# Layer 1 of a two-layer graph and mixture-of-experts kernel: rows kept in token order, pages found by an inverted permutation, and more rules in the event model that orders the instructions

## The chip, the cores and the metric

The program runs on one core of one Trainium2 chip. Its time is the device time of one execution in microseconds (us). The core has TensorE (PE in the profile; PEld is its weight load), VectorE (DVE), ScalarE (ACT), GpSimd (POOL) and SyncE (SP), each with a queue of instructions that it takes in order, and 16 DMA engines that serve SP's queue and POOL's.

## The reference, cut to what matters

Two layers, each a graph attention over 2708 nodes of 256 features and then a mixture of experts in which each node (token) goes to two experts. The change touches the second mixture (16 experts, hidden width 512):

```
x = x + L1_gnn(layernorm(x), adj)
xn = layernorm(x)
logits = xn @ gate_w + gate_b                  # [2708, 16]
topk_vals, topk_idx = top_k(logits, 2)
topk_w = softmax(topk_vals)
h = relu(xn @ w1[e] + b1[e])                   # for the two chosen experts e
moe = sum over the two of topk_w * (h @ w2[e] + b2[e])
x = x + layernorm(xn + moe) * gamma + beta
```

## The kernel before, in words

**Tokens, groups, pages.** The 2708 tokens lie in 22 tiles of 128 rows (the last two hold 74 rows each). In layer 1 they pass the router in four groups, tiles 0 to 5, 6 to 11, 12 to 17 and 18 to 21 (`groups1`). An expert's tokens are gathered in *pages* of 128 rows, each page belonging to one expert; there are at most 58 pages, and the first 45 (`SURE1`) are computed without a test, the others only if they are used. A page is called a block when it is computed, and `where[0]` and `where[1]` say for each block which expert and which page it is.

**Layer 1's attention.** After the projections, for each token tile `i` TensorE sums 22 x 2 matmuls (`sum_up`, L1773) over masks that are stored in fp8 and widened to fp32r by GpSimd or ScalarE, one half of a tile at a time (`widen`, a cast of 128 x 1408 elements, L1621 and L1623). `finish1` and `points1` then make the tile's output `x1`, its layernorm and the normalized row `router1.rows[t]`, a buffer of 259 numbers (256 features, the token's number, a mark of its first expert, and the difference of its two top logits). `logits1` turns two tiles and multiplies them with the gate.

**Routing a group** (`route1`, L2114 on). `pick` finds each token's two experts on VectorE, and GpSimd copies the three trailing numbers into the rows (L671). `rank` counts, by matmuls with triangular and all-one matrices, how many tokens of the same expert come earlier; `number` (VectorE, L710 to L746) turns this into `place`, each token's page and slot as one number. Then `scatter1` (L753) has GpSimd write every tile's rows to their places in DRAM (`rows_d`, 58 x 128 rows), by two indirect DMAs a tile, one for each expert of the token; `plan` (L881 to L948) works out, on VectorE, TensorE and ScalarE, the owners and numbers of the pages that have become full, and the biases.

**The experts** (`Experts.stream`). For each block SP loads the page's 128 rows with one direct DMA at a register's address (`fetch`, L848 to L850) and the expert's weights (L834, L838), unless the block four before had the same expert. TensorE turns the rows (L515), does 16 matmuls for the hidden layer (L972) and nine for the output (L987, L990), ScalarE the relu (L976), VectorE the weight of the token (L964, L994) and the scaled output (L996). GpSimd adds the output's rows to DRAM by an indirect DMA that accumulates (L1001). Blocks of the first group of pages (8 pages, known when tiles 0 to 11 are routed) come first, then 12 pages of tiles 0 to 17, then the rest. The last three blocks are not added in DRAM but joined by matmuls.

**What sets the order.** The instructions of layer 1 from the attention on are emitted in an order that a small event model makes when the program is built (`Clock`): each strand of work is a generator that yields an engine and a duration, or a mark to wait for, and the model always goes on with the strand that can start first, the smaller `urgency` first when two can start together. The order is then fixed; an engine waits in its queue for whatever instruction is at the head. The model knows how long an instruction takes, 0.25 us for a handover between engines, a queue of DMAs, and slots for buffers (13 row buffers `xrs`, five PSUM banks `bank`, three more `acc`, four widened masks). It does not know that SP takes its instructions in order.

Of the kernel before, what the change touches and what calls it, by code (L numbers as in the profile page):

```python
# [64 lines left out]
class Clock:  # L65
# [3 lines left out]
    HANDOVER = 0.25  # L69

    def __init__(self):
        self.now, self.free, self.pieces = 0.0, {}, []

# [21 lines left out]

    def run(self):
        while self.pieces:
            best = None
            for entry in self.pieces:
                ready, urgency, _, want, had = entry  # L100
                if isinstance(want, Mark):
                    if want.at is None:
                        continue
                    key = (max(ready, want.at), -1)
                else:
                    if had not in (None, want[0]):
                        ready += self.HANDOVER
                    key = (max(ready, self.free.get(want[0], 0.0)), urgency)
# [7 lines left out]
            else:  # L116
                entry[4], us, *latency = entry[3]
                entry[0] += us
                self.free[entry[4]] = entry[0]
# [28 lines left out]
def kernel(  # L148
# [381 lines left out]
    for t in (TF, LAST):  # L530
# [12 lines left out]
    tri = filled("tri", 1.0, P, BF16)  # L543
    nc.gpsimd.affine_select(out=tri, in_=tri, pattern=[[1, P]], compare_op=OP.is_gt,
                            fill=0.0, base=0, channel_multiplier=-1)
    ones_bf = filled("ones_bf", 1.0, P, BF16)
# [3 lines left out]
    page_start = counted("page_start", [[0, 1]], 0, P, 1)  # L550
    page_end = counted("page_end", [[0, 1]], P, P, 1)
    of_32 = const.tile([P, 1], F32, name="of_32")
    for k in range(0, P, 32):
        nc.gpsimd.iota(of_32[k:k + 32], pattern=[[0, 1]], base=0, channel_multiplier=1,
                       allow_small_or_imprecise_dtypes=True)
# [13 lines left out]
    class Router:  # L569
# [4 lines left out]
        def __init__(self, layer, E, groups, w_gate, b_gate, pool):  # L574
            self.w_gate, self.b_gate, self.E, self.layer = w_gate, b_gate, E, layer
            self.blocks = NB = blocks_of(E)
            self.rows_d = dram.tile([NB * P, RW], F32, name=f"rows_d{layer}")
# [170 lines left out]

        def scatter(self, t, r):
# [46 lines left out]
    class Experts:  # L796
# [49 lines left out]
        def fetch(self, b):  # L846
            xg = self.xg_tile(b)
            start = nc.values_load(where[1][0:1, b:b + 1], engines=[ET.SP], min_val=0,  # L848
# [13 lines left out]
        def plan(self, upto, bank=None):  # L862

            R, NB, lo, v = self.router, self.NB, self.planned, nc.vector
            E, G, n = R.E, len(R.groups), upto - self.planned

            def small(name, dtype=F32, cols=1):
                return row.tile([P, cols], dtype, name=name, tag=name, bufs=1)[:NB]
# [5 lines left out]
            def give_back(slot):  # L874
                if slot:
# [3 lines left out]
            junk, ones = small("ended", cols=max(len(pairs) * E0, len(groups1) * E1)), ones_bf[:NB]  # L879
            yield SMALL  # L880
            v.scalar_tensor_tensor(junk[:, :G], R.ends[:NB, :, E - 1], page_start[:NB],  # L881
                                   ones[:, :G], op0=OP.is_le, op1=OP.mult, accum_out=whole)
            yield "DVE", 0.2, 0.09
            v.scalar_tensor_tensor(junk[:, :G * E], R.ends[:NB].rearrange("p g e -> p (g e)"),
                                   page_start[:NB], ones[:, :G * E], op0=OP.is_le, op1=OP.mult,
# [5 lines left out]
            if upto == NB:  # L891
                v.tensor_scalar(fresh, self.taken[:NB], -1.0, 1.0, op0=OP.mult, op1=OP.add)
            else:

                open_ = small("open")
                v.scalar_tensor_tensor(junk[:, :E], R.page[:NB], page_end[:NB], ones[:, :E],
                                       op0=OP.is_equal, op1=OP.mult, accum_out=open_)
                yield SMALL
                v.scalar_tensor_tensor(fresh, page_start[:NB], R.ends[:NB, R.done - 1, E - 1:], open_,
                                       op0=OP.is_lt, op1=OP.subtract)  # L900
                yield SMALL
                v.tensor_tensor(fresh, fresh, self.taken[:NB], OP.subtract)
# [5 lines left out]
            nc.tensor.matmul(ps[:NB, :32], tri[:NB, :NB], fresh_bf.to_broadcast([NB, 32]),  # L908
# [3 lines left out]
            v.tensor_scalar(at, ps[:NB, :1], float(lo), None, op0=OP.add)  # L912
            yield "DVE", 0.23, 0.09
            v.scalar_tensor_tensor(sel, self.order[:NB, lo:upto], at, fresh.to_broadcast([NB, n]),
                                   op0=OP.is_equal, op1=OP.mult, accum_out=used)
            v.tensor_tensor(self.taken[:NB], self.taken[:NB], used, OP.add)
            give_back(slot)
            ps, slot = yield from bank_of("where_ps")
            yield "PE", 0.7
            for k, what in enumerate((owner, page_start[:NB])):  # L920
# [1581 lines left out]
```

## Time and profile before

| | us |
|---|---|
| median of 3 runs (lowest, highest) | 1133.14 (1131.94, 1135.37) |
| the profiled execution | 1137.78 |
| its span, first to last instruction | 1136.1 |
| PE busy in the span | 1039.2 (91%) |
| DVE, ACT, POOL busy | 545.7, 577.9, 368.7 |
| DMA moved | 234.38 MB, mean 206 GB/s |

The profile is of one execution. Its second part divides the span into 40 slices of 28.4 us; a digit is the busy share of a slice in tenths, and PEclk is the clock that TensorE was granted, in tenths of full speed. Layer 0's attention fills slices 3 to 11, its experts slices 12 to 23, layer 1's projections slices 24 and 25, its attention slices 26 to 31, the first blocks, beside the routing of the last groups, slices 32 to 34, the other blocks slices 35 to 39, and the last slice is the output. A table by stretches gives for each engine the busy time and, behind an x, the number of instructions. A timeline lists instructions in order of time, like ones merged, with the idle time of the engine before the first of them in brackets, and what ended it: "issue" where the profile shows nothing that it waited for, "remote" where a semaphore ended the wait and no instruction is seen that set it then.

### The profile page before, as it was taken

What the parts mean: (1) busy time and instruction counts of PE and PEld (TensorE: products, weight loads), DVE (VectorE), ACT (ScalarE), POOL (GpSimd) and SP (SyncE); (2) the same over time, 40 slices, a digit from 0 to 9 for tenths busy, and PEclk for the clock granted to TensorE, in tenths of its full rate; (3) what the DMA queues carried; (4) which work ended last, traced back from release to release, by engine and by line L of the source; (5) the groups of instructions that cost most, each with busy time, mean ns of one, the idle gap of its engine ahead of it and who ended that gap; (6) DMA issues with size and microseconds to landing.
All of it is one profiled execution on the core that took longest, in us unless ns stands there. A gap on an engine that the chain in (4) does not pass through costs nothing. (4 is left out here: it accounts for less than half of the span.)

```text
span 1136.1 us, 21474 instructions
## 1 busy us (share of the span) xinstructions
PE 1039.2 (91%) x6707; PEld 922.6 (81%) x6707; DVE 545.7 (48%) x2210; ACT 577.9 (51%) x1602; POOL 368.7 (32%) x425
## 2 busy tenths in 40 slices
PE   5999999998989999999999999898994957999984
PEld 3888888887879999999999954898983846999873
DVE  7788888886431110011001347578775643122257
ACT  4876767665434444444444446445653522444454
POOL 7531113111242211222123271352623155443350
PEclk9999999999989999999999999999997878999998
DMA  9955444431888999999899959301215645685893
GB/s 295 313 211 174 139 175 149 172 94 36 306 256 279 324 325 319 319 325 314 257 311 366 338 156 296 133 1 56 76 39 150 163 145 129 154 208 100 227 315 110
DMA packets 161862, 234.38 MB, mean 206 GB/s; under 512 B 10891, under 2 KB 137798, under 8 KB 159032
## 3 DMA queue, kind: packets, MB, share of 16 engines
q1 hardware_dynamic: 143356, 209.90, 56.0%
q0 software_dynamic: 18384, 23.03, 10.6%
q8 instruction: 56, 0.92, 0.3%
q14 instruction: 66, 0.54, 0.1%
HBM read 205.54 MB, written 54.59 MB: 229 GB/s over the span
## 5 line engine op out<-in xcount | busy, mean ns | idle before, releaser
L996 DVE TENSOR_SCALAR yo<-out_ps,w 128x256 f32<-128x256 f32 x89 | 43.1, 484 | 384.0 <-PE out_ps L990 376.7
L1346 PE MATMUL att_ps<-g_all,z 128*128 128x257 f32 (+3 forms) x968 | 225.3, 385 | 0.0
L1346 PEld LDWEIGHTS att_ps<-g_all,z 128*128 128x128 f32 (+3 forms) x968 | 176.0, 187 | 29.9 <-issue 2.9
L990 PE MATMUL out_ps<-room,ht 128*128 128x256 f32 x840 | 192.0, 381 | 0.0
L972 PEld LDWEIGHTS hid_ps<-xt,room 128*128 128x128 f32 x1504 | 175.8, 193 | 9.6 <-issue 5.0
L972 PE MATMUL hid_ps<-xt,room 128*128 128x128 f32 x1504 | 177.8, 276 | 5.8 <-issue 2.6
L990 PEld LDWEIGHTS out_ps<-room,ht 128*128 128x128 f32 x840 | 155.9, 191 | 20.2
L1332 ACT ACTIVATE zr<-e_bc,minus_one,g_all 128x256 f32<-128x256 f32 (+3 forms) x242 | 130.5, 591 | 41.8 <-DVE z L1335 41.5
L1773 PE MATMUL att_ps<-half,wide_mask 128*128 128x258 f32 (+1 forms) x962 | 130.6, 295 | 14.2 <-issue 7.2
L976 ACT ACTIVATE ht<-hid_ps,w_t 128x128 f32<-128x128 f32 x376 | 128.7, 364 | 28.2 <-PE hid_ps L972 8.3
L1001 POOL DMA_INDIRECT sums<-yo,xg x43 | 66.8, 1554 | 226.9 <-DVE side L964 152.8
L1773 PEld LDWEIGHTS att_ps<-half,wide_mask 128*128 128x128 f32 (+1 forms) x962 | 124.5, 199 | 17.6 <-issue 13.3
L753 POOL DMA_INDIRECT rows_d<-xr,place x88 | 91.7, 1041 | 119.8 <-DVE xr L497 66.5
L1335 DVE SCALAR_TENSOR_TENSOR z<-zr,mask_t 128x256 f32<-128x256 f32 (+3 forms) x242 | 99.1, 428 | 35.1 <-ACT zr L1332 19.1
L976 ACT ACTIVATE ht<-hid_ps,w1x 128x128 f32<-128x128 f32 x180 | 65.0, 366 | 82.5 <-PE hid_ps L972 68.1
L1001 POOL DMA_INDIRECT sums<-yo,xr x42 | 65.3, 1554 | 122.9 <-DMA sums<-yo,xr 34.5
L966 ACT ACTIVATE w<-xg,side 128x1 f32<-128x1 f32 x43 | 12.7, 294 | 163.4 <-DVE side L964 159.5
L1621 POOL CAST wide_mask<-mask_t 128x1408 fp32r<-128x1408 fp8e4 x34 | 47.0, 1388 | 93.1 <-PE att_ps L1773 92.9
L515 PE MATMUL tr_ps<-ident,xr 128*128 128x128 f32 (+1 forms) x214 | 39.3, 294 | 15.3 <-ACT xr L506 13.0
L972 PE MATMUL hid_ps<-lo,wide_mask 128*128 128x128 f32 x368 | 49.5, 290 | 3.5 <-ACT lo L1108 2.9
L972 PEld LDWEIGHTS hid_ps<-lo,wide_mask 128*128 128x128 f32 x368 | 47.9, 205 | 5.7 <-ACT lo L1108 3.9
L515 PEld LDWEIGHTS tr_ps<-ident,xr 128*128 128x128 f32 (+1 forms) x214 | 27.8, 152 | 22.9 <-ACT xr L506 14.3
(334 smaller groups left out, 1450.4 us busy)
## 6 DMA issues: line engine op xcount, KB each, us to landing
room<-in_L_ffn_W_dram SPq DMA_DIRECT2D x94, 1024.0 KB
room<-in_adj_dram SPq DMA_DIRECT2D x20, 1354.0 KB
wide_mask<-in_L_ffn_w_dram SPq DMA_DIRECT2D x46, 512.0 KB
room<-in_L_ffn_w_dram SPq DMA_DIRECT2D x22, 512.0 KB
mask_t<-in_L_ffn_w_dram SPq DMA_DIRECT2D x22, 512.0 KB
rows_d<-nobody SPq DMA_DIRECT2D x1, 7511.0 KB
rows_d<-nobody SPq DMA_DIRECT2D x5, 1295.0 KB
sums<-nobody SPq DMA_DIRECT2D x2, 2944.0 KB
```

Source lines behind the costliest of these rows:

```text
L515: nc.tensor.transpose(ps[:, c, :r], src[:, c * P:(c + 1) * P], ident[:r, :r])
L753: ins = nc.gpsimd.indirect_dma_start(out=self.rows_d[:, :], in_=self.rows[t][:r], in_offset=None, out_offset=bass.IndirectOffsetOnAxis(ap= ...
L972: nc.tensor.matmul(ps[:, :P], w1_b[:, c, f * P:(f + 1) * P], xt[:, c, :], start=(c == 0), stop=(c == DC - 1))
L976: nc.scalar.activation(ht[:, f, :], ps[:, :P], self.func, bias=self.bias[:, f, b:b + 1])
L990: nc.tensor.matmul(ps[:, :D], ht[:, f, :], self.rooms[b % self.deep][1][:, f, :], start=False, stop=(f == self.FC - 1))
L996: nc.vector.tensor_scalar(yo, ps[:, :D], w, None, op0=OP.mult)
L1001: ins = nc.gpsimd.indirect_dma_start(out=self.sums[k][:, :], in_=yo, in_offset=None, out_offset=bass.IndirectOffsetOnAxis(ap=self.rows.pop ...
L1332: nc.scalar.activation(zr[:k, :n], e_bc[:k, lo:lo + n], AF.Relu, bias=minus_one[:k], scale=g_all[:k, j, D + 1:D + 2])
L1335: nc.vector.scalar_tensor_tensor(z[:k, :n], zr[:k, :n], 1.0, mask_t[:k, j // 2, lo:lo + n, j % 2], op0=OP.add, op1=OP.mult)
L1346: nc.tensor.matmul(accs[i][:r, :D + 1], z[:k, q * P:q * P + r], g_all[:k, j, :D + 1], start=(j == 0), stop=(j == LAST))
L1621: nc.gpsimd.tensor_copy(m, src)
L1773: nc.tensor.matmul(accs[i][:, :D + 2], last_masks[i][:k] if late else wide_masks[i, j % 2][:k, j // 2, :], half_k[:k, j, :], start=(j == 0 ...
```

## The change

In layer 1 the rows are no longer scattered. After `pick`, SP stores each tile's row buffers to `rows_d` in token order (`keep`), at the place of the token, with 23 x 128 rows in all; the stores of the normalized rows into `sums1` (`experts1.store`), which were issued in `points1`, are issued in the same place (`store1`). After `number`, VectorE splits the places into page and slot (`places`), and for each tile and each of the two choices builds two 0/1 matrices of 128 columns in bf16 (`mark`): one marks the slot of each token, the other marks the page, its halves multiplied by the tile's number and the row's number. TensorE multiplies them (`invert`, two matmuls a tile), which sums up, for page and slot, the token that lies there; `put` adds this to a table `inv`. `find` picks the blocks' pages out of that table by one fp32 matmul and writes `row_of`, the 128 row numbers of each block (an empty slot gets the number of a row without a token). `fetch` becomes `gather`: GpSimd reads the block's 128 rows from `rows_d` by one indirect DMA. The plan no longer makes `where[1]`. Layer 0 still scatters.

The event model gets three rules: a short VectorE instruction (durations of `SHORT`) that would start in the first 0.55 of a GpSimd cast's time is held until that has passed; TensorE that was idle for over 3.2 us takes 1.9 times as long for the next 8 us; and the cast is an engine use of its own name. Urgencies change: a table `HASTE` moves some strands of the four groups, and `turned`, the token weights and the widening go from 0 to 1.75 or 2. The model's duration of a cast goes from 1.4 to 1.3, and `gather` takes 1.1 of GpSimd.

```diff
+    SHORT, HELD = (0.11, 0.45, 0.5), 0.55
+    IDLE, RAMP, SLOW = 3.2, 8.0, 1.9
...
+    def start_of(self, ready, kind, us):
+        at = max(ready, self.free.get("POOL" if kind == "CAST" else kind, 0.0))
+        return max(at, self.held) if kind == "DVE" and us in self.SHORT else at
+
+    def lasts(self, at, kind, us):
+        if kind == "CAST":
+            self.held = at + us * self.HELD
+        if kind == "PE":
+            if at - self.free.get("PE", 0.0) > self.IDLE:
+                self.cold = at + self.RAMP
+            if at < self.cold:
+                return us * self.SLOW
+        return us
...
-            self.rows_d = dram.tile([NB * P, RW], F32, name=f"rows_d{layer}")
+            self.rows_d = dram.tile([W + P if inverse else NB * P, RW], F32, name=f"rows_d{layer}")
...
+        def keep(self, t, r):
+            g = next(g for g, group in enumerate(self.groups) if group[0][0] <= t <= group[-1][0])
+            for lo, hi in parts_of_rows(r):
+                ins = nc.sync.dma_start(self.rows_d[t * P + lo:t * P + hi, :],
+                                        self.rows[t][lo:hi])
...
+        def places(self, group):
...
+            yield SMALL
+            v.tensor_scalar(page_i, place, 7, None, op0=OP.logical_shift_right)
+            yield SMALL
+            v.scalar_tensor_tensor(slot, page_i, -float(P), place, op0=OP.mult, op1=OP.add)
+            yield SMALL
+            v.tensor_copy(page, page_i)
...
+        def mark(self, group, q, tl):
+            (t, r), (page, slot), v = group[q], self.page_slot, nc.vector
+            marks = tl[:, :D].bitcast(BF16).rearrange("p (k a s) -> p k a s", k=2, a=2)
+            pages = slots[:r, :HALF_P].unsqueeze(1).to_broadcast([r, 2, HALF_P])
+            for k in range(2):
+                j = 2 * q + k
+                v.tensor_scalar(marks[:r, k, 0], slots[:r], slot[:r, j:j + 1], None,
+                                op0=OP.is_equal)
+                v.scalar_tensor_tensor(
+                    marks[:r, k, 1].rearrange("p (h s) -> p h s", h=2), pages, page[:r, j:j + 1],
+                    token[:r, t].unsqueeze(2).to_broadcast([r, 2, HALF_P]), op0=OP.is_equal,
+                    op1=OP.mult)
+            return marks
+
+        def invert(self, group, q, marks, ps):
+            r = group[q][1]
+            for k in range(2):
+                nc.tensor.matmul(ps[:, :P], marks[:r, k, 1], marks[:r, k, 0], start=q + k == 0,
+                                 stop=q == len(group) - 1 and k == 1)
+
+        def put(self, ps):
+            nc.vector.scalar_tensor_tensor(self.inv, ps[:, :P], weight, self.inv, op0=OP.mult,
+                                           op1=OP.add)
...
+        def gather(self, b, xg):
...
+            ins = nc.gpsimd.indirect_dma_start(
+                out=xg, in_=R.rows_d[:, :], out_offset=None,
+                in_offset=bass.IndirectOffsetOnAxis(ap=R.row_of[:, b:b + 1], axis=0))
...
+            if R.inverse:
+                bank.clock.set(routed)
+                bank.clock.start(self.find(lo, upto, sel, bank, inverted), urgency)
...
+        def find(self, lo, upto, sel, bank, inverted):
...
+            nc.tensor.matmul(ps, R.inv, sel, start=True, stop=True)
...
+            v.tensor_scalar(empty, ps, 0.0, own_row, op0=OP.is_equal, op1=OP.mult)
...
+            v.scalar_tensor_tensor(R.row_of[:, lo:upto], ps, float(W), empty, op0=OP.add,
+                                   op1=OP.add)
...
             def fetcher():
                 for b in range(NB):
-                    yield self.known_at[stage(b)]
-                    yield self.scattered_at[stage(b)]
+                    yield self.found_at[stage(b)]
+                    yield self.stored_at[stage(b)]
                     if b >= 4:
                         yield hidden_at[b - 4]
                     xr_slots[b] = yield from xrs.get()
+                    yield "POOL", 1.1
                     self.fetch(b)
...
-    def urgency(two):
-        return 1 + groups1.index(group_of(two)) / len(groups1)
+    HASTE = {"logits1": (-1.75, 0.0, 0.0, 0.0), "finish1": (0.0, -1.0, 0.0, 1.75),
+             "points1": (0.0, -0.5, 0.0, 1.75)}
+
+    def urgency(two, what=None):
+        g = groups1.index(group_of(two))
+        return 1 + g / len(groups1) + (HASTE[what][g] if what in HASTE else 0.0)
...
-        clock.start(scatter1(group, upto), urgency(group))
+        clock.start(invert1(group, inverted_at[g]), urgency(group))
         if upto:
-            yield from experts1.plan(upto, bank)
-        clock.set(routed_at[g])
-
-    def scatter1(group, upto):
+            yield from experts1.plan(upto, bank, inverted_at[g], routed_at[g], urgency(group))
+        else:
+            clock.set(routed_at[g])
+
+    def store1(group, upto):
...
         for t, r in group:
-            yield "POOL", 2.6
-            router1.scatter(t, r)
-            clock.set(xr_slots.pop(t))
-        if upto:
-            clock.set(experts1.scattered_at[upto], 3.5)
+            experts1.store(t, r, router1.rows[t][:r, :D])
+            clock.moved(there, 0.4, 1.0)
+            router1.keep(t, r)
...
+            clock.set(xr_slots.pop(t), 3.0)
```

## The prediction

> **What bounds the kernel now.** I read the page's slices first.
>
> ```profile
> PE   5999999998989999999999999898994957999984
> ...
> PEclk9999999999989999999999999999997878999998
> ```
>
> TensorE is full nearly everywhere; the hole is slices 31 to 34, about 850 to 965 us, where its clock falls too. So the change must be priced there. The table by stretches cuts that hole at its gaps (busy us and counts of PE, PEld, DVE, ACT, POOL, then clock, DMA share, GB/s):
>
> ```profile
> 720.00:855.00 135.00, 123.60 (x993) 121.33 (x992) 94.47 (x424) 72.18 (x183) 59.22 (x59) 0.95 0.12 39
> 855.00:868.00 13.00, 4.78 (x26) 3.99 (x26) 3.79 (x27) 3.52 (x14) 7.43 (x8) 0.70 0.44 132
> 868.00:886.00 18.00, 8.59 (x39) 7.43 (x39) 13.32 (x75) 7.71 (x22) 1.21 (x1) 0.59 0.59 157
> 886.00:917.00 31.00, 28.76 (x210) 26.44 (x209) 19.40 (x141) 16.55 (x53) 11.74 (x16) 0.92 0.55 155
> 917.00:928.00 11.00, 0.00 (x0) 0.00 (x0) 3.81 (x20) 1.50 (x7) 7.16 (x7) 0.71 0.37 106
> 928.00:963.00 35.00, 27.84 (x169) 24.50 (x169) 12.96 (x73) 10.54 (x34) 16.99 (x17) 0.80 0.61 158
> 963.00:1075.00 112.00, 111.81 (x786) 105.32 (x787) 25.71 (x101) 54.36 (x179) 44.01 (x29) 1.00 0.69 165
> ```
>
> In 855 to 868 and 917 to 928 PE, DVE and ACT are all nearly idle and only POOL works: no compute engine bounds these stretches. From 963 TensorE is full, a block every 3.84 us. The timeline of the first stretch, POOL's first and last scatter, then PE, then ACT:
>
> ```profile
> 849.65 0.97 POOL L753 DMA_INDIRECT rows_d<-xr,place  x1 [1.47 <-DVE stat L379]
> ...
> 863.61 0.96 POOL L753 DMA_INDIRECT rows_d<-xr,place  x1 [0.30 <-issue]
> ```
> ```profile
> 858.89 1.05 PE L943 MATMUL bias_ps<-hot_f,w1x 16*128 16x8 f32 x8 [2.95 <-issue]
> 859.88 0.60 PE L1773 MATMUL att_ps<-half,wide_mask 128*128 128x258 f32 x2
> 861.19 0.38 PE L1773 MATMUL att_ps<-half,wide_mask 128*128 128x258 f32 x1 [0.71 <-issue]
> 863.31 0.38 PE L1773 MATMUL att_ps<-half,wide_mask 128*128 128x258 f32 x1 [1.74 <-issue]
> 865.46 0.38 PE L1773 MATMUL att_ps<-half,wide_mask 128*128 128x258 f32 x1 [1.78 <-issue]
> 866.88 3.58 PE L1773 MATMUL att_ps<-half,wide_mask 128*128 128x258 f32 x15 [1.04 <-issue]
> 878.99 2.16 PE L515 MATMUL tr_ps<-ident,xr 128*128 128x128 f32 x8 [8.53 <-ACT xr L506]
> ```
> ```profile
> 858.37 0.21 ACT L925 CAST where<-where_ps 1x8 int32<-1x8 f32 x2 [4.84 <-remote]
> 867.19 0.19 ACT L948 COPY w1x<-bias_ps 128x32 f32<-128x32 f32 x1 [5.99 <-remote]
> ```
>
> Twelve scatters run back to back (0.97 us, 0.30 us apart). After the third or fourth, every other engine creeps: `where_ps` was finished at 853.1, yet ACT starts its copy at 858.37, and PE issues single matmuls 2 us apart although their data are there. One of SP's register moves in this stretch took 715 ns; the median is 29. The same picture stands at 809 to 815 (ACT waits 6.3 us, "remote"), 918 to 928 and, weaker, 953 to 963: the four runs of scatters. Layer 0 scatters four at a time and PE is 25.00 of 25 us busy there. I read: a long run of scatters delays the others' signals, whatever carries them.
>
> **The change part by part.**
>
> *Scatters out.* 44 indirect DMAs of about 1.28 us leave POOL, in runs of 12, 12, 12 and 8. What goes with them on PE:
> - Run 1: 1.02 + 0.93 us idle at 813 and 815; 2.78 at 829, where an accumulator is late because ACT stood; cold matmuls after it (12 in 2.80 us instead of 12 x 0.121 = 1.45, and a gate of 1.42 instead of 0.96), 1.8. Sum 6.5.
> - Run 2: 2.95 + 0.71 + 1.74 + 1.78 + 1.04 = 8.2 idle, and 15 cold matmuls in 3.58 instead of 1.8. Sum 10.0.
> - The 8.53 us before 878.99 wait for normalized rows whose DVE chain stood 3.5 and 5.1 us in run 2. That chain is the last to end here, so the 8.6 us move it one for one: I take 8.
> - Run 3: PE stands 11.25 us at 917 (a bias matmul waits for a bank, the bank for ACT, ACT for a signal), then nine cold matmuls cost 1.9. What is late next is the pages themselves: places at about 909, now 15.4 us of scatters, a landing and a fetch behind; in the new form 6 us of marks and a gather. I take 9 of 13.
> - Run 4: 1.39 + 1.37 idle at 958 and 962. I take 2.
> Together 35.5.
>
> *Marks, inversion, find.* On DVE four instructions a tile, 88 in all. None is in the trace; the nearest rows are 128x96 compares, 0.26 us (0.17 from start to start), and 128x192 ones, 0.36. By these a tile costs 0.7 to 1.4; I take 0.8, near the 96-column row, since 128 is nearer to 96: 18 us, and 3 us for the 12 + 4 + 6 small ones. DVE is 65 to 75% busy here, and POOL's casts stretch some of its short instructions to 1.2 us and more, so there is no full cover: the first two groups' marks lie under attention, those of groups 3 and 4 (10 tiles, 8 us) lie in the chain to the pages, half of it beside the plan's own matmuls and copies. I charge 5 (bounds 1 and 14). On PE 44 bf16 matmuls: the rank's rows do ten in 0.60 and twelve in 0.45, so 0.06 to 0.25 each (the last if weights of 128 columns don't overlap); at 0.1 it is 4.4, all charged, as PE is the bound. The three fp32 products of `find` replace the three of `page_start` (0.36 us): nothing.
>
> *Gathers in, fetches out.* 45 SP fetches leave SP's queue, each with a register load and checks of about 1.5 us before its DMA; 45 gathers enter POOL's. No gather is in the trace. From below it costs a scatter's 0.97, from above an add's 1.55; I take 1.0, the same rows and one index each. Per block POOL then has 1.55 + 0.30 + 1.0 + 0.30 = 3.15 of 3.84 us: it fits, with 0.7 to spare, and if it costs 1.55 it fits with 0.14. Queued behind a gather that waits are the adds, and behind these only the last sums. So in the full stretch nothing. At the end it helps: the last fetches sit in SP's order behind weight loads, one of them takes 7.46 us in the chain that ended last, and PE stands 2.12 and 4.02 us at 1077 and 1087 (DMA share 1.05). POOL's queue is not behind the weights; the DMA engines are still shared. I take 3 of 6.
>
> By the Trainium skill, page "SBUF — State Buffer", section "Who interferes with whom", VectorE in a two-port mode locks GpSimd out of the port through which it writes descriptors, and such DMAs should go to a hardware queue: a rule against this change, which adds bf16 compares and moves 45 loads to POOL. The trace's 88 scatters took 0.96 to 1.39 us, median 0.98, beside a DVE that was mostly busy; by the rule the sum would lose up to that 0.4 us a gather, most of it under PE.
>
> *Stores.* 22 tiles of rows in token order, 24 SP issues of 0.37 us = 9 us, more than paid by the fetches' 45 x 1.5. But they and the moved `sums1` stores wait at SP's head for POOL's copies (L671), and `x_d` and weight loads queue behind: bounds 0 and 6 (two groups by 3 us of POOL's casts); I take 0. The smaller fill (23 x 128 rows instead of 58 x 128) lies at 683 to 715, under projections and attention that don't wait for it: 0.
>
> *Event model.* It now knows held DVE instructions and cold matmuls. The gap at 774 to 778.7 (4.43 idle, 1.6 cold) is one that it had misjudged, with DVE instructions stretched under casts before it; nothing in the trace prices a new order, which can also lose: bounds -6 and +6; I take a gain of 3.
>
> Sum: 35.5 + 3 + 3 - 4.4 - 5 = 32. The profiled execution took 1137.8 (span 1136.1 and 1.7 around it), 4.6 over the median of 1133.1; 1137.8 - 32 = 1105.7, on the median's scale 1101.
>
> **The rivals.**
> - *A, as above*: 1101, own range 1083 to 1114. For it: three engines idle together exactly in the runs of scatters.
> - *B, the chain becomes the bound.* The stalls go but pages of groups 3 and 4 come no earlier, because DVE, 65 to 75% busy, now has 21 us more and its chain of points, pick, number, marks is what is late. Then only runs 1 and 2 are won, 16.5 - 4.4 = 12: 1121, 1114 to 1129. Against it: DVE was idle 7 of 11 us and 22 of 35 us in the stretches of runs 3 and 4.
> - *C, it does not do what it says*: the creeping is not the scatters' doing but comes with each burst of routing, and stays; the other terms cancel (3 + 3 - 4.4 - 5 = -3): 1136, within 0.3% or little over.
> - *D, slower: gathers stall signals as scatters do.* POOL's DMA instructions then fill 2.55 of each 3.84 us all through the 43 blocks, against 0.96 of 1.27 us in the runs that stall and 1.54 of 3.84 in the stretch that doesn't. If each block loses more than 32 / 43 = 0.75 us, the change loses; one delayed signal, SP's 0.7, and some of a second, 1.1 us a block, gives 1101 + 47 = 1148. Against it: layer 0's runs of four do no harm, and gather and add alternate with a pause.
>
> **How the numbers follow.** A 0.57, B 0.2, C 0.06, D 0.17. A's, B's and part of C's range make up 8 in 10: 1082 to 1138; A's low end leaves little out, as the whole loss of TensorE in the hole is about 55 us. A measurement of this kernel tells 0.3%, 3.4 us, from no change. Faster by more: A, B and a little of C, 0.77; within: 0.05; slower: D and some of C, 0.18.
>
> **What would show it.** Right: no stretch after 800 us with PE, DVE and ACT idle together while POOL issues; ACT's "remote" waits gone; attention ends near 855 instead of 870; the full stretch begins near 930 instead of 963. Gathers of about 1.0 us, a block still 3.84 us. B: the creeping gone, but PE waits for row gathers or for `row_of` between blocks 7 and 12. C: single matmuls 2 us apart without scatters. D: blocks of 4.6 us and more, "remote" waits in the full stretch. I am wrong in kind if POOL's queue, an add waiting at its head with a gather behind it, starves TensorE.

## The result and the profile after

The changed kernel takes **1162.57 us** (median of 4, 1160.08 to 1163.45), the kernel before beside it 1132.54 (1130.48 to 1135.37): ratio **1.0247**, 95% interval 1.0221 to 1.0273. It is slower by 30 us; the forecast was 1101. The profiled execution took 1161.93, span 1160.2.

The slices of the changed kernel's page:

```profile
PE   5999999999999999999999998999968998666784
...
PEclk9999999999999999999999999999979989999887
```

The hole of before, slices 31 to 34, has shrunk to a 6 and an 8 in slices 30 and 31 (841 to 899 us). A new one is open in slices 35 to 38 (from 986 us on, three 6 and a 7), where before was full. The table by stretches (busy us and counts of PE, PEld, DVE, ACT, POOL, then clock, DMA share, GB/s) says what kind of hole:

```profile
900.00:940.00 40.00, 37.67 (x252) 33.19 (x251) 21.08 (x116) 16.85 (x53) 20.32 (x21) 0.88 0.67 177
940.00:970.00 30.00, 30.00 (x210) 27.79 (x210) 4.66 (x21) 13.10 (x44) 15.15 (x13) 1.00 0.62 164
970.00:1000.00 30.00, 20.71 (x128) 18.25 (x128) 3.85 (x15) 7.81 (x26) 11.03 (x9) 0.94 0.49 111
1000.00:1030.00 30.00, 19.47 (x131) 16.74 (x131) 5.32 (x20) 9.01 (x30) 13.19 (x10) 1.00 0.26 41
1030.00:1060.00 30.00, 20.62 (x125) 17.80 (x125) 5.31 (x20) 8.61 (x29) 12.82 (x10) 0.94 0.36 79
```

From 940 to 970 TensorE is full, with gathers and adds side by side, some 20 us earlier than in the profile of before. Then, suddenly, a third of it is idle although no other engine is half busy, and the DMA engines are at 0.26 to 0.49. Nothing is short of throughput: something waits. The waits after 960, by engine (waiter, what it waited for: us in total, times, longest):

```profile
PE hid_ps L1105 <- ACT lo L1242: 47.3, 20, 5.4
```
```profile
DVE yo L1129 <- DMA sums<-yo,xr: 103.1, 19, 7.0
```
```profile
POOL xr L964 <- DMA sums<-yo,xr: 31.7, 8, 4.8
POOL xr L964 <- PE out_ps L1123: 29.0, 9, 4.9
```

TensorE waits for ScalarE, VectorE for buffers (`yo`) that adds still read, and POOL's **gathers** (L964) wait too. POOL's timeline in that stretch:

```profile
1000.77 1.03 POOL L964 DMA_INDIRECT xr<-rows_d,row_of  x1 [2.98 <-PE out_ps L1123]
1002.11 1.59 POOL L1134 DMA_INDIRECT sums<-yo,xr  x1 [0.31 <-issue]
1006.67 1.04 POOL L964 DMA_INDIRECT xr<-rows_d,row_of  x1 [2.97 <-PE out_ps L1123]
1008.01 1.59 POOL L1134 DMA_INDIRECT sums<-yo,xr  x1 [0.30 <-issue]
1012.58 1.03 POOL L964 DMA_INDIRECT xr<-rows_d,row_of  x1 [2.98 <-PE out_ps L1123]
```

Each add starts right behind a gather, and each gather stands still for 3 us first. Counted back from the last one, the gather at 1006.67 is that of page 32, and the add behind it that of page 20. The row buffers are a ring of 13: gather 32 overwrites page 19, whose add, issued at 1002.11, still reads its token numbers from there. The semaphore of that add, for which the gather waits, is complete at 1005.84 in the trace, 3.73 us after the issue. (The bracket names TensorE as the releaser, but the gather starts 0.83 us after the landing. It does so again at 1025.95, where the landing came late, 5.2 us after the issue, and there the profile names the add.) So the loop is add, 3.73 us to its landing, 0.83 to the gather's start, 1.04 and a pause of 0.30, next add: 5.9 us, and it turns in POOL's queue alone. In other turns the landing took up to 5.6 us. Blocks follow the loop: 16 of them from 974.69 to 1079.03 take 6.52 us on average, against 3.84. That is 43 us.

This is not the order in which the code issues them. There gather 32 follows add 25, when the buffer has long been free (the run `behind` below has this order). But line 195 keeps the written order for PE, ACT, DVE and SP only; POOL's queue is ordered by the framework. In the trace each gather of this stretch stands directly behind the add that frees its buffer, ahead of the next six adds that the code had put first. In the profile of before the same buffers were filled from SP's queue, where no add stands; between 960 and 1075 its loads (L850) waited four times there, at most 0.4 us, and for ScalarE, not for a landing.

### The profile page after: what moved, and what is told of

Read it like the earlier page. It is cut to its first block, busy times and chain, and to the rows that moved or that the text cites. A ratio compares the mean times of both kernels' runs of the same rounds, so it can differ in the third digit from the quotient of the medians.

```text
span 1160.2 us, 21413 instructions
## 1 busy us (share of the span) xinstructions
PE 1047.9 (90%) x6751; PEld 921.6 (79%) x6751; DVE 562.6 (48%) x2320; ACT 577.4 (50%) x1599; POOL 370.9 (32%) x436
## 5 line engine op out<-in xcount | busy, mean ns | idle before, releaser
L1907 PE MATMUL att_ps<-half,wide_mask 128*128 128x258 f32 (+1 forms) x962 | 125.1, 288 | 4.0 <-DVE wide_mask L1925 2.0
L1907 PEld LDWEIGHTS att_ps<-half,wide_mask 128*128 128x128 f32 (+1 forms) x962 | 119.1, 191 | 6.3 <-issue 2.1
L1109 ACT ACTIVATE ht<-hid_ps,w1x 128x128 f32<-128x128 f32 x180 | 62.6, 363 | 75.3 <-PE hid_ps L1105 64.3
L964 POOL DMA_INDIRECT xr<-rows_d,row_of x45 | 45.2, 1005 | 109.4 <-DMA sums<-yo,xr 37.4
L848 POOL DMA_INDIRECT rows_d<-xr,place x44 | 47.1, 1070 | 98.9 <-DVE xr L516 66.5
L1105 PE MATMUL hid_ps<-lo,wide_mask 128*128 128x128 f32 x368 | 54.6, 307 | 26.5 <-ACT lo L1242 26.5
L1105 PEld LDWEIGHTS hid_ps<-lo,wide_mask 128*128 128x128 f32 x368 | 50.7, 217 | 30.9 <-ACT lo L1242 30.4
L1099 ACT ACTIVATE w<-xr,side 128x1 f32<-128x1 f32 x45 | 13.1, 292 | 86.9 <-DVE side L1097 86.7
```

Of the source, the lines that this page charges most:

```text
L848: ins = nc.gpsimd.indirect_dma_start(out=self.rows_d[:, :], in_=self.rows[t][:r], in_offset=None, out_offset=bass.IndirectOffsetOnAxis(ap= ...
L964: ins = nc.gpsimd.indirect_dma_start(out=xg, in_=R.rows_d[:, :], out_offset=None, in_offset=bass.IndirectOffsetOnAxis(ap=R.row_of[:, b:b + ...
L1105: nc.tensor.matmul(ps[:, :P], w1_b[:, c, f * P:(f + 1) * P], xt[:, c, :], start=(c == 0), stop=(c == DC - 1))
L1109: nc.scalar.activation(ht[:, f, :], ps[:, :P], self.func, bias=self.bias[:, f, b:b + 1])
L1907: nc.tensor.matmul(accs[i][:, :D + 2], last_masks[i][:k] if late else wide_masks[i, j % 2][:k, j // 2, :], half_k[:k, j, :], start=(j == 0 ...
```

## The experiments

Theories: **T1**, POOL's order makes the loss; **T2**, POOL's DMA instructions stall signals (rival D); **T3**, the model's rules make the difference in the hole. Two came up on the way: **T5**, on some chips signals or instructions come late, whatever POOL does, and **T6**, the `yo` buffers are the bound. Runs named together ran on one chip. There, the kernel before did not always take 1133 us: on four chips 1101 to 1102, on a fifth 1134. I call these the **first** and the **second kind**; the prediction's profile is of the second. Every run is compared with the kernel before on its own chip.

**The order (first kind).**

`behind`, and once more as `behind_again` and `behind_third`: a gather is ordered behind the last adds written before it.

```diff
+            for last in self.last_add.values():
+                tc.add_manual_dep(ins.ins, last.name, mybir.DependencyInfo(
+                    mybir.DependencyClass.NoSync, mybir.DependencyReason.DATA),
+                    reason="adds come first")
```

> The changed kernel, with each gather bound to stand behind the last adds that were written before it in POOL's order (an order alone, no semaphore). T1, the queue order: in the changed kernel's trace the gather of page b stands directly ahead of the add of page b-12 and waits for the landing of the add of page b-13, so that each block lasts add issue to landing 3.7 + gather 1.0 + pauses, about 5.9 us. With the adds first the gather waits for nothing late; blocks of 3.84 us all the way, TensorE's 47 us of idle time between 970 and 1120 mostly gone: 1162.6 - 47 = 1115 us, between 1100 and 1125. T2, gathers and adds together stall signals (my rival D): the same DMA instructions in another order, so blocks of 5 to 6 us stay and the time is 1150 to 1165.

Measured 1100.94 us, the kernel before 1101.39: ratio 0.9993 (0.9979 to 1.0006). Its POOL timeline:

```profile
1000.02 1.58 POOL L1138 DMA_INDIRECT sums<-yo,xr  x1 [0.97 <-DVE yo L1133]
1001.91 0.99 POOL L964 DMA_INDIRECT xr<-rows_d,row_of  x1 [0.30 <-ACT lo L1246]
1003.87 1.58 POOL L1138 DMA_INDIRECT sums<-yo,xr  x1 [0.97 <-DVE yo L1133]
```

The same instructions at the same price, now 3.84 us apart, and POOL waits for work, 0.97 us before each add. What the order cost needs the changed kernel on the same chip:

> The changed kernel, unedited, beside the others of one chip. T1: the block of about 5.9 us comes from POOL's order and the landing of an add, which no chip escapes: 47 us above the run with the gathers behind the adds. T5 alone: the change loses what it loses only on a chip that creeps, and here it stands within 10 us of the kernel before.

> The run with the gathers behind the adds once more, for the same chip as the unedited two. T1: 47 us under the changed kernel. Against the kernel before: on a chip without remote waits equal within 3 us, as measured; on one with them (T5 and my prediction's sum together) 20 to 30 us faster.

Changed kernel 1150.25, mended order 1101.53, kernel before 1101.45: ratios 1.0444 (1.0406 to 1.0482) and 0.9997 (0.9979 to 1.0014). The order alone costs **48.7 us**; 47 were expected. Taking away the wait instead of the order (`own_index`):

```diff
+                own = self.pool.tile([P, 1], I32, name="own_d", bufs=8)
+                nc.vector.tensor_copy(own, xg[:, D:D + 1].bitcast(I32))
...
-                out_offset=bass.IndirectOffsetOnAxis(ap=self.rows.pop(b)[:, D:D + 1].bitcast(I32),
-                                                     axis=0), compute_op=OP.add)
+                out_offset=bass.IndirectOffsetOnAxis(ap=index, axis=0), compute_op=OP.add)
```

> The changed kernel with POOL's order left as the framework makes it, but the add takes its token numbers from a small copy (one 128x1 instruction of VectorE a block), so that a page's row buffer is free once TensorE, VectorE and ScalarE have read it; the gather no longer waits for the landing of an add. T1 by its second half, that the wait for the landing is what makes the block long: the gather stays ahead of an add in POOL's order but waits for reads that are over, so blocks of about 3.84 to 4.2 us and 1115 to 1125 us. If the position alone did it (any gather ahead of an add) or if the DMA instructions stall signals (T2), 1150 to 1165.

Measured 1100.08, ratio 0.9988 (0.9974 to 1.0002), better than expected.

```profile
998.85 1.59 POOL L1140 DMA_INDIRECT sums<-yo,own_d  x1 [0.96 <-DVE yo L1134]
1000.74 0.99 POOL L965 DMA_INDIRECT xr<-rows_d,row_of  x1 [0.30 <-ACT lo L1247]
1002.69 1.59 POOL L1140 DMA_INDIRECT sums<-yo,own_d  x1 [0.96 <-DVE yo L1134]
```

Counted as above, gather 32 stands even ahead of add 18 here. Gathers may stand ahead of adds: what hurts is a gather that waits for an add's landing. Two different cuts through one loop give the same time, so T1 holds. The largest wait in the changed kernel's list was VectorE's for `yo`. Is it the cause? `yo3` makes these buffers scarcer (more don't fit):

```diff
-            yo = self.pool.tile([P, D], F32, name="yo", bufs=4)
+            yo = self.pool.tile([P, D], F32, name="yo", bufs=3)
```

> The changed kernel, POOL's order left as it is, with three buffers for the weighted outputs (yo) instead of four. In the changed kernel's waits the largest is VectorE's for a yo buffer, 81.5 us for the landing of adds. T1: the block of 5.9 us is made in POOL's queue (landing of an add, gather, next add) and the wait for yo only hands it on, so one buffer less leaves the time within 4 us of the changed kernel's. T6, the yo buffers are the bound: three in place of four lengthen the block, 10 to 40 us slower.

Measured 1154.02 beside 1100.83, ratio 1.0497 (1.0464 to 1.0529), 0.5% more than the changed kernel's ratio on another chip: some 6 us, over T1's 4 and under T6's 10, but the two intervals overlap. POOL's loop is all but unmoved:

```profile
1001.79 1.59 POOL L1134 DMA_INDIRECT sums<-yo,xr  x1 [0.31 <-issue]
1006.44 1.03 POOL L964 DMA_INDIRECT xr<-rows_d,row_of  x1 [3.06 <-PE out_ps L1123]
1007.78 1.61 POOL L1134 DMA_INDIRECT sums<-yo,xr  x1 [0.30 <-issue]
```

5.99 us from add to add. So the longest wait in the list was a victim; the gathers' waits, in the loop that sets the pace, came to 31.7 and 29.0 us there. Last, more DMA instructions on POOL (`behind_twice`):

```diff
+            again = nc.gpsimd.indirect_dma_start(
+                out=dram.tile([W + P, RW], F32, name="spare_rows", bufs=4)[:, :], in_=nobody, in_offset=None,
+                out_offset=bass.IndirectOffsetOnAxis(ap=R.row_of[:, b:b + 1], axis=0))
```

> The run with the gathers behind the adds, and behind each gather a scatter of 128 unused rows to spare rows in DRAM that nothing reads, so POOL has 1.0 + 1.0 + 1.6 and three pauses of 0.3 = 4.5 us of DMA instructions in each block of 3.84. POOL becomes the bound: in 30 of the blocks 0.66 us each, 10 to 30 us slower, with TensorE waiting for gathers or buffers. If DMA instructions of POOL hold up the others' signals (my rival D), more than 40 us slower, and remote or issue waits on ScalarE, VectorE and TensorE in the full stretch.

Measured 1115.18, ratio 1.0127 (1.0098 to 1.0155), 14 us slower: within what a full POOL should cost.

```profile
1002.32 1.60 POOL L1142 DMA_INDIRECT sums<-yo,xr  x1 [0.30 <-issue]
1004.22 1.00 POOL L966 DMA_INDIRECT xr<-rows_d,row_of  x1 [0.30 <-ACT w L1107]
1005.52 0.97 POOL L974 DMA_INDIRECT spare_rows<-nobody,row_of  x1 [0.30 <-issue]
1006.80 1.61 POOL L1142 DMA_INDIRECT sums<-yo,xr  x1 [0.31 <-issue]
```

POOL needs 4.48 us a block without a break, TensorE still runs blocks of 3.84 until the gathers' lead is used up at about 1010, and no remote wait appears on ScalarE, VectorE or TensorE. T2 is out on this kind of chip.

**The scatters, on both kinds.** With the order mended nothing was won on the first kind; where are the 35.5 us?

> The kernel before, unedited, for its trace beside the others of one chip. The profile that my prediction read had ScalarE and TensorE waits that the profile names remote or issue, 16.6 us and more, in the runs of scatters; the four kernels run so far had none of them, in before_model's long runs of scatters neither, and the kernel before took 1101 us beside them instead of 1133. If the scatters make the engines creep (my prediction's first step), these waits are in this trace too. If the chip makes them (T5: on some chips signals or instruction supply are late, whatever POOL does), the trace has none where the time is 1101 us, and 30 us less idle time of TensorE between 780 and 965.

Measured 1100.98, ratio 0.9988 (0.9971 to 1.0006), and no remote wait at all. TensorE, then POOL, in the second run of scatters:

```profile
845.24 2.90 PE L1773 MATMUL att_ps<-half,wide_mask 128*128 128x258 f32 x22
848.07 1.05 PE L943 MATMUL bias_ps<-hot_f,w1x 16*128 16x8 f32 x8
849.05 2.67 PE L1773 MATMUL att_ps<-half,wide_mask 128*128 128x258 f32 x20
```
```profile
841.85 0.97 POOL L753 DMA_INDIRECT rows_d<-xr,place  x1 [1.47 <-DVE stat L379]
...
855.78 1.19 POOL L753 DMA_INDIRECT rows_d<-xr,place  x1 [0.30 <-issue]
```

The same twelve scatters, 0.30 us apart, and TensorE runs beside them without a gap; attention ends at 851.7, 18.8 us earlier than in the prediction's trace. SP's register moves took at most 42 ns here, up to 715 there. So on this kind of chip a run of scatters holds nothing up. Breaking the runs there (`before_gaps`) can only delay the pages:

```diff
+                    if len(self.moves) % 3 == 0:
+                        for _ in range(8):
+                            pause = nc.gpsimd.memset(filler["tile"], 0.0)
```

> The kernel before with eight memsets of a 128x256 tile on POOL (about 2.5 us) behind every third scatter of layer 1, so that no run of scatters is longer than three. If long runs of scatters hold up the other engines' signals, the remote waits go where the kernel before has them, and the time falls or, as the runs take twice as long, stays within 10 us. If the scatters do nothing to the signals, the remote waits stay where the kernel before has them, and where it has none the time rises by what the later landing of the pages costs: 14 pauses of 2.5 us, of which the first two groups' lie under attention, so 5 to 20 us.

Measured 1116.4, ratio 1.0128 (1.0095 to 1.016): 15.0 us slower, as expected of late pages. One set of runs fell on the second kind, the kernel before at 1133.88:

```diff
-            for k in range(2):
+            for k in range(2 - self.layer):
```

> The kernel before without the scatters of the second choice in layer 1: 22 of its 44 scatters are left out, so half of the pages' rows are empty ones, and the runs are of 6, 6, 6 and 4. My prediction put 35.5 us on the 44 scatters, most of it on signals held up from the third or fourth scatter of a run on: 12 us or more off the kernel before. If on a chip without remote waits the scatters cost only the later landing of the last pages (T5; the pauses behind scatters came to 15.0 us for 35 us of pauses): the last groups' pages come about 7.7 and 5 us earlier, half of it to be seen, 3 to 8 us off. If they lie under other work: within 3 us.

Measured 1109.8, ratio **0.977** (0.9734 to 0.9806): 24 us off for half of the scatters. Its ScalarE waits, where the prediction's trace had 6.3, 6.0, 5.3 and 4.8:

```profile
ACT wide_mask L1623 <- remote: 4.8, 1, 4.8
ACT where L925 <- remote: 4.0, 2, 3.2
```

The run leaves out the scatters of the second choice, so pages also land earlier, which the expectation put at 3 to 8 us at most; two thirds of the 24 are left. Runs of six hold up less than runs of twelve. On the second kind the scatters do make the engines creep, and not those of layer 1 alone. At 315 to 329 in the prediction's trace, eight scatters of layer 0 and an add stand almost without a break, and ScalarE waits beside them:

```profile
318.79 0.29 ACT L966 ACTIVATE w<-xn,side 128x1 f32<-128x1 f32 x1 [3.80 <-issue]
```

TensorE is busy 9.97 of these 14 us, against 13.81 in `before_again`. The same wait of 3.80 us stands in this run's trace and in those of `behind_split` and `behind_pool` below, all of the second kind; the changed kernel's trace lacks it, but TensorE is busy only 11.32 of the 14 us there.

**The rules and the marks.**

`behind_oldmodel` (mended order, the model's rules, table and urgencies taken back), and the reverse, `before_model` (the kernel before with these alone), on one chip of the first kind:

> As the run with the gathers behind the adds, but with the event model's new rules, the HASTE table and the urgencies of 1.75 and 2 taken back: the inverse and the gathers alone. T1 with my prediction's sum (scatters out 35.5, tail fetches 3, matmuls and marks -9.4): the hole between 850 and 965 is closed by the scatters' removal, not by the new order, so within 6 us of the run with the new rules either way. T3, the rules close the hole (and the scatters were not what made the engines creep): 15 us or more slower than the run with the rules, with ScalarE's remote waits of 4 us and more back.

> The kernel before with the event model's new rules, the HASTE table and the urgencies alone; scatters and fetches as before. My prediction's step: a gain of 3 us, bounds 6 either way, 1127 to 1139. T3, the rules close the hole: 1105 to 1120. The creeping in the runs of scatters (single matmuls 2 us apart, remote waits of 4 to 6 us on ScalarE) must still be there if the scatters make it.

1112.46, ratio 1.0108 (1.0087 to 1.0129), and 1096.04, ratio **0.9956** (0.9939 to 0.9973). The inverse without the rules costs 11 us there; rules, table and urgencies together win 5.4 without it and 11.5 with it. Neither theory had this: the rules don't close a hole, but the inverse needs the new order. The rules without table and urgencies (`before_rules`):

> The kernel before with the event model's rules alone (held VectorE instructions, cold matmuls, the cast's own kind), without the HASTE table and the urgencies of 1.75 and 2. The rules and the table together took 5.4 us off the kernel before. If the rules do it, 1094 to 1098; if the table and urgencies do it, 1099 to 1104. It is also the smallest edit that might beat both kernels.

1100.11, ratio 0.9993 (0.9979 to 1.0007): the rules alone win nothing, so table and urgencies do it, by themselves or with the rules. What does the inverse cost? `marks2` writes the marks twice:

```diff
-            for k in range(2):
+            for k in (0, 1, 0, 1):
```

> The run with the gathers behind the adds, and VectorE writes each tile's four mark instructions twice (the same values, 88 more instructions of 285 and 342 ns, 27 us of VectorE). If the marks are on the path that sets the end, as half of those of groups 3 and 4 in my prediction, 4 to 12 us slower; if all of the inverse's instructions lie on it, up to 27; if attention and the first pages cover them, within 3 us.

1122.25, ratio 1.0191 (1.0163 to 1.0219). On this chip the mended kernel itself was not run; as it equals the kernel before on three others, the doubling cost about 21 us for 18.7 of VectorE. Then marks meant to be cheaper, on the second kind, the last also with the slot marks moved to POOL:

```diff
-                v.scalar_tensor_tensor(
-                    marks[:r, k, 1].rearrange("p (h s) -> p h s", h=2), pages, page[:r, j:j + 1],
-                    token[:r, t].unsqueeze(2).to_broadcast([r, 2, HALF_P]), op0=OP.is_equal,
-                    op1=OP.mult)
+                for h, weighs in enumerate((float(t - T), own_row[:r])):
+                    v.tensor_scalar(marks[:r, k, 1, h * HALF_P:(h + 1) * HALF_P],
+                                    slots[:r, :HALF_P], page[:r, j:j + 1], weighs,
+                                    op0=OP.is_equal, op1=OP.mult)
```

> The run with the gathers behind the adds, and each page mark of two halves is written by two 64-column instructions with two scalars instead of one 128-column one that reads a third operand (262 ns from start to start; a 128-column compare with one scalar takes 162, so two of 64 columns about 190 to 200). 44 times 65 ns is 2.9 us less of VectorE. Doubled marks (18.7 us more from start to start) cost 20.7 us, so if VectorE is the bound of the routing stages, 2 to 4 us off the run with the gathers behind the adds, 1097 to 1099; if the doubling cost so much for another reason (the event model didn't know of it), within 1.5 us of that run.

> As behind_split, and the 44 slot marks are written by POOL instead of VectorE: 44 x 162 ns = 7.1 us less of VectorE, and some 0.3 to 0.5 us each, 13 to 22 us, more of POOL, which the scatters have left (it was 30 percent busy from 780 to 900). If VectorE bounds the routing stages: 6 to 10 us off the run with the gathers behind the adds, 1091 to 1096. If POOL's queue, in which the marks now stand before casts, gathers and adds, is what is late next: no gain, or slower.

`behind_split` 1109.86, ratio **0.9789** (0.9763 to 0.9815); `behind_pool` 1116.31, ratio 0.9851 (0.9823 to 0.9878): a slot mark took POOL 781 ns in the mean, VectorE 287, and TensorE now waits up to 5.7 us for POOL's marks. Both expectations were set against 1101 us and are void as absolute times. But the first says much: **on the second kind the change with its order mended (and split marks) is 24 us faster than the kernel before.** With the order's 43 to 48.7 us that makes the changed kernel 19 to 25 us slower there; measured were 30. The order alone was not measured on the second kind, and the 5 to 11 us between are not explained. The last set came on the first kind again, the kernel before at 1101.92:

> The run with the gathers behind the adds, on whatever chip comes. Two kinds have been seen: on three chips the kernel before takes 1101 us and this run 1101 to 1102; on the fourth, as on the chip of the prediction, the kernel before takes 1133 to 1134. T1 and T5 together: on a chip of the first kind 1099 to 1103; on one of the second the changed kernel's 1162.6 less the 48.7 us that the order cost, 1114, some 20 us faster than the kernel before.

> The gathers behind the adds and the page marks in two 64-column instructions, once more. If VectorE's time in the routing stages sets the time, 2 to 4 us under the run beside it whose marks are as in the changed kernel; if not, within 1.5 us of it.

> The kernel before with the event model's new rules, the table and the urgencies, once more, as it was the fastest on the first kind of chip (1096). On a chip of the first kind 1094 to 1098. On one of the second the scatters still hold up the signals, so 1115 to 1135, and slower than the run with the gathers behind the adds if the scatters' runs are what costs there.

1101.7, 1104.21 and 1098.59; ratios 0.9992 (0.9967 to 1.0016), 1.001 (0.9983 to 1.0038) and 0.996 (0.9938 to 0.9981). The split marks are not faster, and the trace says why: from start to start the two 64-column instructions took 146 and 206 ns, 352 together, where the one they replace took 262. My expectation had their price wrong; the edit adds 4.0 us of VectorE, and the time rose by 2.5, which is within the noise. More work on the marks was slower clear of noise once, 21 us for 18.7. No run made them cheaper.

`split_again` is the kernel of `behind_split` and has none of layer 1's scatters. It differs by 5.7 us between the two kinds (1104.21 and 1109.86); the kernel before differs by 32.0 (1101.92 and 1133.88). As an estimate, then, some 26 of these 32 us go with what the change takes out.

The best version measured is the kernel before with the model's rules, table and urgencies on the first kind (1096 to 1099, 0.4% under both kernels there), and the mended change with split marks on the second. How the mended change with its own marks and `before_model` stand on the second kind, and the changed kernel beside these, was not run.

## Why the prediction was wrong, point by point

- **"Gathers in, fetches out … Queued behind a gather that waits are the adds, and behind these only the last sums. So in the full stretch nothing." This step failed.** The gather's price was right (1.005 us against 1.0), and POOL's 3.15 us a block do fit into 3.84, as the mended run shows. But I asked for how long POOL is busy, not for what a gather waits and who stands behind it. It waits for an add's landing, 3.7 us and more; the next add stands behind it; behind the adds stand four `yo` buffers, then VectorE, ScalarE and TensorE, all in order. Measured: 48.7 us on the first kind, instead of 0; in the second kind's trace 16 blocks lose 43. The prediction's last sentence named POOL's queue but the mirror image, an add at its head with a gather behind.
- *"Scatters out … 35.5."* The reading, that a long run of scatters delays the others, holds on the kind of chip it was read from: half of the scatters gone gave 24 us on a chip of that kind. It is no property of scatters as such: the traces from four other chips show none of it. The argument from layer 0 ("four at a time and PE is 25.00 of 25 us busy there") holds for 225 to 250; at 315 to 329 TensorE lost 4 of 14 us beside eight scatters. In the changed kernel's own trace the signs that I asked for came: ScalarE's remote waits are gone (two waits of 3.3 us, named issue, are left at 930 and 939), attention ends at 848.8 (855 was forecast, 870.5 before), and the stretch from 940 is full (930 was forecast). The size is not measured alone; the estimate above is 26 us, and with all other terms it came to 24 with the mended order and split marks, against 32 in the sum.
- *"Marks … I charge 5 (bounds 1 and 14)."* Their duration was right (0.85 us a tile from start to start against 0.8). The charge was too low: doubled marks cost 1.1 us of time for each us of VectorE, which would make the 18.7 us cost 21. This is an estimate from making them dearer, and rather a high one, for it also holds what the event model, which did not know of the extra work, orders badly.
- *PE, "at 0.1 it is 4.4".* The 44 products took 0.230 us each in the mended kernel, at the upper bound of 0.25, and TensorE is 10.1 us busier than in the kernel before on the same chip (1039.7 and 1029.6). Of the two rows that the bounds came from, twelve in 0.45 give 0.04 each, so the low bound of 0.06 was too high.
- *"At the end it helps … I take 3 of 6."* It came: the long steps between the last blocks are 6.2 and 5.5 us in the mended run, 7.5, 5.6 and 5.5 in the kernel before on the first kind, 4.1 and 7.1 us over 3.84 a block in all. But from the end of TensorE's last expert matmul to the end of the span the mended runs take 34.4 to 35.7 us, the kernel before 31.1, `before_model` 32.4 and `behind_oldmodel` 34.0. No term of the sum has these 3 to 5 us; the rules and the inverse each seem to add a part, and why is not shown.
- *"Event model … a gain of 3."* 5.4 and 3.3 without the inverse, inside the bounds; with it 11.5, outside.
- *Stores and fill at 0*: not tried by themselves. A fetch took SP 0.8 us ahead of its DMA (988.67 to 989.48 in the prediction's trace), not 1.5; 45 of them still outweigh the 9 us of stores.
- *The rule of the Trainium skill, "SBUF — State Buffer", "Who interferes with whom"*: 45 gathers took 0.98 to 1.01 us in the mean in every run. One gather of the changed kernel stands beside VectorE's bf16 marks, and it took 1.00 us. No run shows the price that the rule would put on them.
- *Rivals.* D gave the right sign by the wrong mechanism: the same density of DMA instructions runs at 3.84 us a block in another order, on the second kind too (TensorE 80.00 of 80 us busy from 960 to 1040 in `behind_split`). VectorE still waits four times after 960 there without a cause to be seen, up to 3.2 us each, but TensorE in that stretch loses nothing by it. C's number fits the first kind of chip, where the mended kernel wins 0.0, but not C's reason: there is no creeping there that could stay. B's sign did not come: TensorE nowhere waited long for gathers or `row_of`. B's reason, that VectorE's marks are late next, is in part what `marks2` shows.

Open stays what differs between the two kinds of chips, by what path scatters hold up signals on the second, and what the marks cost by themselves. Each chip was used in one sitting only, so the runs can't tell either whether the kind belongs to the chip or to something that lasted through the sitting.

## What to carry to other kernels

When a DMA moves to another queue, write down for each instruction what it waits for, what stands behind it, and whether these are the same resource: a load that waits at the head of an in-order queue for a transfer which the instruction behind it must follow turns that transfer's latency into the period of the loop. Check who orders that queue; an order written in the code is none if the framework may reorder the engine. And a stall that no instruction explains should be looked for on a second chip before a change is priced by it.

## What the runs showed of the hardware that was not expected

- One program took 1101 to 1102 us on four chips and 1132 to 1134 on others, single runs within 1% of the median of their chip. On the slow ones the traces have waits without a cause to be seen, of 1.5 to 6.3 us, 3 to 13 in each; elsewhere there is one in all (2.9 us, `after_again`); SP's register moves, 29 ns in the median everywhere, reach 511 to 715 ns there and at most 42 ns elsewhere.
- In the loop of the changed kernel the landing of an add of 128 rows came 3.7 to 3.9 us after its issue in over half of the turns and up to 5.6 in the others, though POOL is free after 1.59.
- A 128x128 bf16 compare with one scalar took VectorE 162 ns from start to start, a 128x64 one with two scalars 146 (one a constant) or 206 (both from memory): half of the columns saved little or nothing. POOL needed 781 ns for the first.
